# Graph network, one core: block 21 of layer 1 fetched instead of counted, and team pairs of layer 2 moved ahead

## The chip, the cores and the metric

The kernel runs on one core of one Trainium2 chip. The metric is the device time of one execution in microseconds (us), the median over runs. Lower is better.

## The reference

Three graph-convolution layers over 6250 nodes and 100,000 edges (plus one loop per node), then a residual and a layer norm. `norm_edge` is the product of the two ends' `dinv`, so each layer is: scale the rows, sum them over a node's incoming edges, scale again, multiply by a weight matrix, add a bias, relu.

```python
h = x
for W, b in ((W1, b1), (W2, b2), (W3, b3)):      # 256->512, 512->512, 512->256
    h = relu(segment_sum((h @ W)[src] * norm_edge[:, None], dst, num_segments=n) + b)
return layernorm(x + h)
```

## The kernel before

**Blocks, and two ways to sum.** The 6250 nodes are 50 blocks (`NB`) of 125 rows (`Q`). The edges come sorted by destination, so a block's incoming edges are a run of up to 16 chunks of 128 (`KF`). The neighbours' rows of a block are summed in one of two ways.

- *Fetched* ("gathered"): GpSimd (POOL in the profile) issues one indirect DMA per chunk (`gather`, line 1306) that brings 128 source rows, and TensorE (PE) adds them up with a one-hot matrix (`product`, line 1334). Where a row was stored as its fp32r high half and low half side by side (table `both`), one chunk is one matmul over 512 columns. VectorE (DVE) makes the one-hot matrices, four chunks at a time (line 1246), and the last matmul of a block takes the few edges beyond 16 chunks.
- *By count matrix* ("dense"): PE first makes a matrix that holds how many edges lead from each node to each node of the block (`counts`, line 878, from comparisons on DVE in line 811; the banks are copied out as bytes by ScalarE, ACT, in line 840). Then 50 matmuls of 125x125 by 125x512 sum the block (line 1407), one for every block of sources. ACT turns five such 125x125 pieces at a time from bytes to fp32r (line 1255).

Count matrices are made once, in layer 1, for 29 blocks (`MANY`): they are stored to memory and used again in layers 2 and 3.

**Steps.** Each layer is one loop over *steps* in `layer`. A step issues one gather, the product of the gather some steps back, up to three dense matmuls, and whatever the listed generators (`extras`, `going`) have to do in that step. A `yield n` in a generator means "go on n steps later". This order is fixed when the program is built, and each engine runs its part of it in order. Layer 1 is index 0 in the code, layer 2 index 1, layer 3 index 2.

**Layer 1** (451 steps, and a few without a gather at the end). The first 22 blocks (`FEW`) are dense, 28 are fetched; the fetched blocks from `BOTH_FROM` = 26 on come from the table `both`, into 12 row buffers. The dense matmuls are spread over the steps by `spacing`: a block per 19 steps, and never over three matmuls in a step. The count matrices are made in the order of the blocks, with the seven that only later layers use put in behind blocks 3, 6, 9, ... (`EXTRAS_AFTER`). Each summed block goes through `after1`: scale, transpose, W1 (line 1452), bias and relu, and a store to the table of layer 2.

**Teams.** Blocks 0 to 11 of layer 2 are summed by count matrices as three *teams* of four blocks (`teams`). The sum is held transposed in four banks, one a block; for a source block k and a bank, one *pair* of matmuls (high half and low half of k's rows, line 1005) adds its part. There are 3 x 50 x 4 = 600 pairs. They need the rows of layer 2's input, streamed in two blocks at a time (a load for every eight pairs), split by ACT (line 960) and DVE (line 962), and the count pieces, which are loaded and turned to fp32r by ACT (line 952). The pairs begin in layer 1 once the dense blocks are finished, three pairs in two steps, and go on in layer 2: three a step in its first nine steps, then 24 pairs in 23 steps (`PACE`). Counted from the code, the loads for the teams are issued from step 431 on, the first pair stands in step 444, 29 pairs stand in layer 1 and 571 in layer 2, and the last one is in step 532 of layer 2. When a team is complete, DVE scales its four banks (`scaled`, line 940), and `hidden` runs them through W2 and W3.

**Layer 2** (612 steps). Blocks 12 to 49 are fetched, 2 KB a row, into seven row buffers. ACT splits off the high half (line 1366), DVE the low half (line 1371), which sets the row buffer free for the next gather; PE then takes both halves (two matmuls a chunk). `after2` and `hidden` turn two blocks at a time through W2 (line 1513) and W3 (line 1533). Layer 2's first gather needs all of layer 2's table, so it waits for the last block of layer 1 to be stored.

**Layer 3** (322 steps) sums 30 blocks by count matrices and fetches 20.

```python
if in_layer == 0 and pairs_done % 3 or in_layer == 1 and (pairs_done % PACE if now >= EAGER else pairs_done % 3 == 0):
    yield 1
...
until = min(len(work), int((chunk + 1 - first) * NB / spacing))
if i == 0:
    until = min(until, done + 3)
```

Of the kernel before, what the change touches and what calls it, by code (L numbers as in the profile page):

```python
# [31 lines left out]
SOON = 2  # L32
LATE = 6
# [5 lines left out]
SPLIT_ROWS = (12, 9, 20)  # L39
LOANED = 3  # L40
EAGER = 9
PACE = 24
LANDING = 8
AT_ONCE = 3
RETURN = 6
# [5 lines left out]
COUNTING = 3  # L51


FEW = 22
BOTH_FROM = 26
BOTH_LAG = 5
SPLIT = ((0, 0, BOTH_LAG), (1, 2, 8), (0, 0, 10))
EXTRAS_AFTER = (3, 6, 9, 11, 13, 15, 17)
TEAM = 4
TEAMS = 3  # L60
HOME = 17
# [347 lines left out]
def sorted_path(ctx: ExitStack, tc: tile.TileContext, x, edges, starts, found, wts, biases, room, late, out):  # L409
# [60 lines left out]
    def free(name, bank=None):  # L470
        held[name] -= 1
        if name in idle:
            idle[name].append(bank)

    def take(name, most):
        while held.get(name, 0) >= most:
            yield 1
        held[name] = held.get(name, 0) + 1
# [316 lines left out]
    def counts(blocks, places):  # L795
# [4 lines left out]
        def place_for(n):  # L800
            for place in places:
                last = owner.get(id(place))
                if last is None or (last in stored if last >= FEW else last < finished):
                    owner[id(place)] = blocks[n]
# [21 lines left out]
        def copied(now_on):  # L826
            while whole and whole[0][0] <= now_on:
# [5 lines left out]
                stored.add(blocks[n])  # L833
                if blocks[n] < FEW:
                    there.append(now + 1)
# [80 lines left out]
    def teams(groups):  # L916
# [14 lines left out]
        def load(p):  # L931
            if 2 * p < len(units):
                k = units[2 * p][1]
                by_rows(nc.sync, streamed[p % RING], tables[1][k * Q:(k + 2) * Q, :].rearrange("(b p) c -> p b c", p=Q))

        def load_scales(g):
            nc.sync.dma_start(out=scales, in_=dinvs[g * TEAM:(g + 1) * TEAM, :].rearrange("b p -> (b p)").unsqueeze(0).to_broadcast([P, TEAM * Q]))

        def scaled(g, n):
            nc.vector.tensor_tensor(team_zt[:, n], team_banks[n][:, :TEAM * Q], scales, op=ALU.mult)  # L940
            free(f"team{n}")
            if n == TEAM - 1:
                if g + 1 < len(groups):
                    load_scales(g + 1)
                yield SOON
                team_ended[0](hidden(groups[g][:2], team_zt[:, :, :2 * Q], "tz"))
                for _ in range(4 * KF if g + 1 < len(groups) else 2 * KF):
                    yield 1
                team_ended[0](hidden(groups[g][2:], team_zt[:, :, 2 * Q:], "tz"))
# [13 lines left out]

        while products < FEW * NB - HOME // PIECE * PIECE:
            yield 1
# [5 lines left out]
        load_scales(0)  # L971
        while finished < FEW:
            yield 1
# [13 lines left out]
        pairs_done = 0  # L987
        for u, (g, k) in enumerate(units):
            if u == len(units) - RETURN:
                returning = now  # L990
            if u % 2:
                load((u + 1) // 2 + RING - 1)
            for n in range(TEAM):
                if k == 0:
                    yield from take(f"team{n}", 1)
                if k == NB - 1 and n == 0:
                    while held.get("tz", 0):
                        yield 1
                    held["tz"] = TEAM // 2
                if 1 <= n < 3:  # L1000
                    half(u + 2, n - 1)
                if k % PIECE == 2 and u + PIECE < len(units):
                    piece(*divmod(g * CUTS + k // PIECE + 1, CUTS), n)
                for h in range(2):
                    nc.tensor.matmul(team_banks[n][:, :TEAM * Q], lhsT=both_parts[u % 3][:, h * HID + n * P:h * HID + (n + 1) * P],
                                     rhs=team_pieces[(g * CUTS + k // PIECE) % 2][:, k % PIECE, :],
                                     start=(k == h == 0), stop=(k == NB - 1 and h == 1))
                if k == NB - 1:
                    team_ended[0](scaled(g, n))
                pairs_done += 1  # L1010
                if in_layer == 0 and pairs_done % 3 or in_layer == 1 and (pairs_done % PACE if now >= EAGER else pairs_done % 3 == 0):
                    yield 1
        teams_done = True
        assert not on_loan, (now, len(on_loan))
# [142 lines left out]
    def layer(i, width, gathered, dense, after, rows, first=0, spacing=1.0, extras=(), carried=None):  # L1157
# [110 lines left out]
        def of_both(c):  # L1268

            n, b, _ = items[c]  # L1270
            return i == 2 or i == 0 and (n * GRP if b is None else b) >= BOTH_FROM

# [14 lines left out]
        def gather(c):  # L1287
            nonlocal turn
            n, b, j = items[c]
            table = both_halves if i == 0 and of_both(c) else tables[i]  # L1290
            if (i, b, j) == (0, BOTH_FROM, BOTH_LAG + 1):
                hot_stores.appendleft(late_hot_room)
# [313 lines left out]
    now = in_layer = products = 0  # L1606
    few, many, every = list(range(FEW)), list(range(MANY)), list(range(NB))

# [13 lines left out]
    def steps(b):  # L1622

        return (NB - b) * KF + NG - b // GRP
# [8 lines left out]
            yield 1  # L1633

    first = 16
    spacing = 19.0
    made_in_order = []
    for b in few:
        made_in_order.append(b)
        if b in EXTRAS_AFTER:  # L1640
            made_in_order.append(FEW + EXTRAS_AFTER.index(b))
    assert sorted(made_in_order) == many
# [30 lines left out]
    spacing = (steps(len(most)) - SOONER) / (len(most) - BEGUN * PIECE * len(ADVANCE) / NB)  # L1673
# [182 lines left out]
```

## Time and profile before

| what | value |
|---|---|
| median of 3 runs | 2067.19 us (2065.59 to 2067.45) |
| profiled execution, its own time | 2064.83 us |
| its span, first to last instruction | 2063.2 us |
| busy PE / DVE / ACT / POOL | 1926.2 / 1379.0 / 1279.3 / 1381.4 us |
| moved by DMA | 535.53 MB, mean 260 GB/s |

Layer 1's gathers run from 74 to 684 us of the span, layer 2's from 708 to 1615, layer 3's from 1646 to 2049.

In the rows of the profile, "PE" is a matmul, "PEld" the load of its weights, which overlaps other matmuls; matmuls are pipelined too, so the time from the start of one to the start of the next says what it costs, and its own duration does not. In the rows by windows, the number behind x is how many instructions overlap the window. In the timeline, a row is start, duration, engine, line, operation, what it writes and reads, and in brackets the idle time before it with what ended it. A row of waits is: who waited for whom, us in total, times, longest.

### The profile page before, as it was taken

What the parts mean: (1) busy time and instruction counts of PE and PEld (TensorE: products, weight loads), DVE (VectorE), ACT (ScalarE), POOL (GpSimd) and SP (SyncE); (2) the same over time, 40 slices, a digit from 0 to 9 for tenths busy, and PEclk for the clock granted to TensorE, in tenths of its full rate; (3) what the DMA queues carried; (4) which work ended last, traced back from release to release, by engine and by line L of the source; (5) the groups of instructions that cost most, each with busy time, mean ns of one, the idle gap of its engine ahead of it and who ended that gap; (6) DMA issues with size and microseconds to landing.
All of it is one profiled execution on the core that took longest, in us unless ns stands there. A gap on an engine that the chain in (4) does not pass through costs nothing. (4 is left out here: it accounts for less than half of the span.)

```text
span 2063.2 us, 29141 instructions
## 1 busy us (share of the span) xinstructions
PE 1926.2 (93%) x8679; PEld 1521.4 (74%) x8679; DVE 1379.0 (67%) x2443; ACT 1279.3 (62%) x2255; POOL 1381.4 (67%) x1425
## 2 busy tenths in 40 slices
PE   4399999999999789999999989999889999999997
PEld 3277777777777557778888868888768778788886
DVE  6887888887882376677687676767746445444444
ACT  2566777787875466666676666666656555555553
POOL 2467777766777377777676676766757277777775
PEclk9999999999999899999999999999989999999998
DMA  7898999999999998999999998998997599999997
GB/s 171 246 300 220 264 266 259 272 264 254 276 274 248 250 280 255 267 262 265 263 263 265 263 261 249 267 254 253 266 278 221 151 288 292 289 294 299 290 284 203
DMA packets 266078, 535.53 MB, mean 260 GB/s; under 512 B 44363, under 2 KB 80328, under 8 KB 265910
## 3 DMA queue, kind: packets, MB, share of 16 engines
q0 software_dynamic: 155280, 355.58, 63.3%
q1 hardware_dynamic: 97194, 168.45, 30.3%
q10 hardware_dynamic: 13436, 9.55, 1.8%
q8 instruction: 70, 1.15, 0.2%
q14 instruction: 98, 0.80, 0.1%
HBM read 459.56 MB, written 73.87 MB: 259 GB/s over the span
## 5 line engine op out<-in xcount | busy, mean ns | idle before, releaser
L1306 POOL DMA_INDIRECT room<-tab,ssrc x442 | 456.4, 1033 | 199.8 <-issue 86.2
L1334 PE MATMUL sacc<-halves,shot 128*125 128x512 f32 x1524 | 519.9, 402 | 9.7 <-DMA halves<-tab,ssrc 4.7
L1255 ACT CAST piece<-room 125x625 fp32r<-125x625 uint8 x492 | 350.8, 721 | 187.4 <-PE win_ps L1407 53.0
L1306 POOL DMA_INDIRECT halves<-both,ssrc x384 | 360.5, 939 | 141.9 <-issue 42.4
L1306 POOL DMA_INDIRECT halves<-tab,ssrc x320 | 303.2, 947 | 98.8 <-issue 29.2
L1334 PEld LDWEIGHTS sacc<-halves,shot 128*125 128x125 f32 x1524 | 287.1, 189 | 84.3 <-DVE halves L1371 7.5
L811 DVE TENSOR_TENSOR back<-near_cols,slots 128x625 bf16<-128x625 f32 (+2 forms) x435 | 325.0, 803 | 31.5 <-PE sacc L878 12.4
L1371 DVE TENSOR_TENSOR halves<-room,halves 128x512 fp32r<-128x512 f32 x334 | 226.8, 692 | 121.2 <-ACT halves L1366 118.8
L1246 DVE TENSOR_TENSOR shot<-near_cols,sdlo 128x500 fp32r<-128x500 f32 x366 | 244.9, 670 | 93.2 <-PE sacc L1334 87.6
L1306 POOL DMA_INDIRECT back<-tab,ssrc x230 | 230.9, 1004 | 112.9 <-DVE halves L1371 35.1
L1366 ACT CAST halves<-room 128x512 fp32r<-128x512 f32 x334 | 202.0, 620 | 137.8 <-DMA room<-tab,ssrc 127.8
L1513 PE MATMUL win_ps<-back,w_sb 128*128 128x250 f32 x768 | 183.3, 382 | 9.1 <-ACT back L1490 8.6
L1513 PEld LDWEIGHTS win_ps<-back,w_sb 128*128 128x128 f32 x768 | 148.5, 194 | 33.5 <-ACT back L1490 11.0
L1407 PE MATMUL smm<-parts,piece 125*125 125x512 f32 x565 | 165.9, 409 | 2.1 <-DVE parts L1563 1.2
L1407 PE MATMUL win_ps<-parts,piece 125*125 125x512 f32 x550 | 158.2, 406 | 0.0
L1407 PE MATMUL str<-parts,piece 125*125 125x512 f32 x515 | 149.5, 408 | 0.9 <-ACT piece L1255 0.9
L878 PEld LDWEIGHTS <-back 128*125 128x125 bf16 x725 | 95.9, 138 | 73.3 <-issue 23.0
L1407 PE MATMUL sacc<-parts,piece 125*125 125x512 f32 x450 | 147.7, 432 | 0.9 <-ACT piece L1255 0.9
L840 ACT CAST room<-sacc 125x500 uint8<-125x500 f32 (+1 forms) x155 | 107.7, 713 | 55.3 <-PE sacc L878 40.8
L1371 DVE TENSOR_TENSOR halves<-back,halves 128x512 fp32r<-128x512 f32 x136 | 93.3, 693 | 61.1 <-ACT halves L1366 60.4
L1407 PE MATMUL mat_ps<-parts,piece 125*125 125x512 f32 x415 | 121.3, 408 | 0.4 <-ACT piece L1255 0.4
L962 DVE TENSOR_TENSOR parts<-parts 125x512 fp32r<-125x512 f32 x150 | 103.0, 687 | 25.5 <-ACT parts L960 24.8
(353 smaller groups left out, 3477.5 us busy)
## 6 DMA issues: line engine op xcount, KB each, us to landing
parts<-tab SPq DMA_DIRECT2D x75, 448.0 KB
kept<-room SPq DMA_DIRECT2D x29, 683.6 KB
room<-kept SPq DMA_DIRECT2D x27, 683.6 KB
both<-parts SPq DMA_DIRECT2D x10, 1120.0 KB
tab<-st SPq DMA_DIRECT2D x50, 224.0 KB
own_row<-tab SPq DMA_DIRECT2D x38, 224.0 KB
parts<-kept SPq DMA_DIRECT2D x60, 136.7 KB
room<-tab,ssrc POOLq DMA_INDIRECT x442, 6.2
```

The lines of the kernel that those rows point to most:

```text
L811: nc.vector.tensor_tensor(out, near_cols[:, :shape[2]].unsqueeze(1).to_broadcast(shape), numbers.unsqueeze(2).to_broadcast(shape), op=ALU. ...
L840: nc.scalar.copy(place[:, :, u * G:(u + len(ms)) * G].rearrange("p k (t r) -> p t k r", r=G), counted_in[:Q, :len(ms) * 256].rearrange("p ...
L878: nc.tensor.matmul(bank[:Q, len(pair) * 256:][:, :G * NB], lhsT=hot_lo, rhs=hot_key, start=True, stop=True)
L962: nc.vector.tensor_sub(to[:, HID:], row, to[:, :HID].bitcast(F32))
L1246: nc.vector.tensor_tensor(hot[:, :n], near_cols[:, :Q].unsqueeze(1).to_broadcast([P, n, Q]), dlo.rearrange("p b j -> p (b j)")[:, at:at + ...
L1255: nc.scalar.copy(piece[:, :n], made_or_read[:, at:at + n, :])
L1306: nc.gpsimd.indirect_dma_start(out=row, out_offset=None, in_=table, in_offset=bass.IndirectOffsetOnAxis(ap=at, axis=0))
L1334: nc.tensor.matmul(acc[:Q, :size], lhsT=hot, rhs=row[:, c0:c0 + size], start=(i != 0 and k == c0 == 0), stop=(k == KF and c0 + size == row ...
L1366: nc.scalar.copy(halves[:, :width], landed[highs])
L1371: nc.vector.tensor_sub(halves[:, width:], landed.pop(lows), halves[:, :width].bitcast(F32))
L1407: nc.tensor.matmul(acc_d[:Q], lhsT=got[p][:, n, :], rhs=parts[:, k], start=begins and not (i == 2 and m < BEGUN), stop=ends)
L1513: nc.tensor.matmul(h_ps[:, f, :], lhsT=w2_sb[:, k, (f2 + f) * P:(f2 + f + 1) * P], rhs=zt[:, k, :], start=(k == 0), stop=(k == KH - 1))
```

## The change

One block of layer 1, block 21, is fetched instead of summed by its count matrix: 21 dense blocks and 29 fetched ones, 467 steps with a gather instead of 451. `BOTH_FROM` moves with it, so that four blocks are still fetched as plain rows and 25 instead of 24 come from `both`. The count matrix of block 21 is still made, now as the eighth of those for later layers. A dense block is spread over 20 steps instead of 19; 21 x 20 and 22 x 19 are 420 and 418 steps, so the dense blocks end in the same step (435) and the first team pair stands in the same step (444). The 16 further steps lie behind that, with three pairs to two steps: 53 pairs stand in layer 1 and 547 in layer 2. In layer 2, from step 9 on, there is one pair in each step; the last one is in step 530. Behind a finished team, `hidden` of its first two blocks is begun 12 steps after the last scaling instead of 2.

```diff
-FEW = 22
-BOTH_FROM = 26
+FEW = 21
+BOTH_FROM = 25
...
-EXTRAS_AFTER = (3, 6, 9, 11, 13, 15, 17)
+EXTRAS_AFTER = (3, 5, 7, 9, 11, 13, 15, 17)
...
-                yield SOON
+                yield LATE
+                yield LATE
                 team_ended[0](hidden(groups[g][:2], team_zt[:, :, :2 * Q], "tz"))
...
-                if in_layer == 0 and pairs_done % 3 or in_layer == 1 and (pairs_done % PACE if now >= EAGER else pairs_done % 3 == 0):
+                if in_layer == 0 and pairs_done % 3 or in_layer == 1 and (now >= EAGER or pairs_done % 3 == 0):
                     yield 1
...
-    spacing = 19.0
+    spacing = 20.0
```

Three places show how the instructions move. The first is PE in the middle of layer 1, while dense block 4 is summed: `L1407` are the dense matmuls, `L1334` the product of a fetched chunk, `L878` the making of counts. Before:

```order
L878 MATMUL smm<-back 125x250
L1407 MATMUL mat_ps<-parts,piece 125x512 x3
L1334 MATMUL sacc_891<-halves_879,shot_852 125x512
L878 LDWEIGHTS back
L878 MATMUL win_ps<-back 125x250
L1407 MATMUL mat_ps<-parts,piece 125x512 x3
```

Now (line 878 is 877, since a constant is gone):

```order
L1407 MATMUL smm<-parts,piece 125x512 x3
L1334 MATMUL sacc_891<-halves_878,shot_852 125x512
L877 LDWEIGHTS back
L877 MATMUL str<-back 125x250
L877 LDWEIGHTS back
L877 MATMUL sacc_892<-back 125x250
L1407 MATMUL smm<-parts,piece 125x512 x2
```

Two and three dense matmuls now take turns from step to step here, where before three came oftener; elsewhere, where blocks wait for their counts, steps without dense matmuls come in between. The second place is PE at the end of layer 1, at the 18th team pair and what follows: `L1005` is a pair, `L1318` the start of a fetched block, `L1426` a transpose of `after1`. Before:

```order
L1005 MATMUL str<-parts 128x500 x2
L1334 MATMUL win_ps<-halves_880,shot_852 125x512
L1334 MATMUL win_ps<-halves_881,shot_852 125x512
L1005 MATMUL sacc_893<-parts 128x500 x2
L1005 MATMUL mat_ps<-parts 128x500 x2
```

Now, at the same pair:

```order
L1005 MATMUL mat_ps<-parts 128x500 x2
L1005 MATMUL smm<-parts 128x500 x2
L1334 MATMUL sacc_891<-halves_880,shot_853 125x512
L1005 MATMUL str<-parts 128x500 x2
L1334 MATMUL sacc_891<-halves_881,shot_853 125x512
L1426 MATMUL win_ps<-ident_r,szs 128x125 x2
L1005 MATMUL sacc_893<-parts 128x500 x2
L1005 MATMUL mat_ps<-parts 128x500 x2
L1334 MATMUL sacc_891<-halves_870,shot_853 125x512
```

Before, the last products of layer 1 stood there and only pairs and the last block's `after1` came behind them; now a whole fetched block still follows, with the pairs between its products.

The third place is PE in layer 2 at the product of its 19th and 20th chunks (two matmuls each), where the old pace put two pairs in one step. Before:

```order
L1334 MATMUL sacc_892<-halves_6034,shot_853 125x512 x2
L1005 MATMUL str<-parts 128x500 x2
L1005 MATMUL sacc_893<-parts 128x500 x2
L1334 MATMUL sacc_892<-halves_6035,shot_853 125x512 x2
L1005 MATMUL mat_ps<-parts 128x500 x2
```

Now:

```order
L1334 MATMUL sacc_892<-halves_6084,shot_852 125x512 x2
L1005 MATMUL str<-parts 128x500 x2
L1334 MATMUL sacc_892<-halves_6085,shot_852 125x512 x2
L1005 MATMUL sacc_893<-parts 128x500 x2
```

The second pair of that step is gone, and so in every 23rd step of layer 2.

1 line of the change is left out of this document (removed).

## Prediction

> **What bounds the kernel now.** I read the page for its totals, then the windows by stage, then what each engine waits for in a stage, and last the timeline at the end of layer 1, where the change puts its work. First the page, and the windows: layer 1's steady stretch, its end, layer 2's steady stretch, layer 3.
>
> ```profile
> PE 1926.2 (93%) x8679; PEld 1521.4 (74%) x8679; DVE 1379.0 (67%) x2443; ACT 1279.3 (62%) x2255; POOL 1381.4 (67%) x1425
> ```
>
> ```profile
> core 0: us, PE busy (x) PEld busy (x) DVE busy (x) ACT busy (x) POOL busy (x), PEclk, DMA share, GB/s
> 74.00:160.00 86.00, 68.02 (x325) 51.51 (x326) 69.76 (x119) 49.60 (x85) 55.74 (x56) 1.00 0.85 267
> 232.00:640.00 408.00, 402.86 (x1930) 298.51 (x1929) 334.41 (x546) 315.98 (x556) 292.39 (x311) 1.00 0.96 265
> 900.00:1480.00 580.00, 566.69 (x2546) 471.06 (x2545) 424.77 (x676) 387.78 (x713) 404.38 (x395) 0.99 0.92 261
> 1646.00:2050.00 404.00, 401.72 (x1730) 320.66 (x1728) 195.98 (x474) 210.38 (x333) 304.58 (x322) 1.00 1.16 286
> ```
>
> PE is busy almost throughout in all three, but a busy PE may still be waited for or not, so the steps and the waits decide. The same windows for the gathers alone count the steps, and the waits of POOL in layer 1 say what holds them:
>
> ```profile
> 232.00:640.00 408.00, 288.74 (x308) 1.00 0.96 265
> 1646.00:2050.00 404.00, 304.58 (x322) 1.00 1.16 286
> ```
>
> ```profile
> POOL halves L1306 <- PE sacc L1334: 14.3, 30, 1.4
> POOL halves L1306 <- PE sacc L878: 14.1, 31, 2.0
> ```
>
> Layer 1 takes 408/308 = 1.325 us a step. Layer 3 takes 404/322 = 1.255, and the timeline of POOL shows why no layer can go below that by much: gathers that nothing holds up start 1.24 us apart (674.55, 675.79).
>
> ```profile
> 655.50 0.94 POOL L1306 DMA_INDIRECT halves<-both,ssrc  x1 [0.30 <-PE smm L1334]
> ...
> 674.55 0.94 POOL L1306 DMA_INDIRECT halves<-both,ssrc  x1 [0.30 <-issue]
> 675.79 0.94 POOL L1306 DMA_INDIRECT halves<-both,ssrc  x1 [0.31 <-issue]
> ...
> 684.37 0.94 POOL L1306 DMA_INDIRECT halves<-both,ssrc  x1 [2.67 <-DMA parts<-tab]
> 708.49 1.01 POOL L1306 DMA_INDIRECT room<-tab,rest  x1 [23.18 <-ACT parts L960]
> ```
>
> So in layer 1 PE sets the pace (POOL's waits name PE, which hands the row buffers back), 0.08 us a step above POOL's floor; in layer 3 PE and that floor lie together; and between 684.37 and 708.49 POOL has nothing to do until the last block of layer 1 is through.
>
> **The change, term by term.** The profiled execution took 2064.83 us, 2.4 below the median of 2067.19; the sum is made against the former and 2.4 is added at the end.
>
> *First term: 50 dense matmuls leave layer 1's steady stretch.* What one costs shows where nothing else is between them:
>
> ```profile
> 637.01 0.40 PE L1334 MATMUL sacc<-halves,shot 128*125 128x512 f32 x1
> 637.24 0.87 PE L1407 MATMUL win_ps<-parts,piece 125*125 125x512 f32 x3
> 637.96 0.39 PE L1334 MATMUL sacc<-halves,shot 128*125 128x512 f32 x1
> ```
>
> Four matmuls of 512 columns in 637.96 - 637.01 = 0.95 us: 0.235 each, not the 0.39 of the row. 50 x 0.235 = 11.7 us. The dense work ends in the same step (435), so this comes off the same number of steps. Up to about step 58 PE is not full (68 of 86 us in the window from 74), and 43 x (50/19 - 50/20) = 6 of the 50 fall there; 44 x 0.235 = 10.3. Spread over 377 steps that is 0.027 a step, to 1.298, still above 1.24, so POOL's floor does not take it back. I take -10; bounds -5 (if half of the steps without a dense matmul run into that floor) and -11.7. The ten casts to fp32r that go from ACT, and the gather rate that rises by 2% from 265 GB/s where layer 3 moves 286, I cost at nothing: neither ACT nor the transfers hold PE there.
>
> *Second term: 16 more steps at the end of layer 1*, each with a gather of 256 KB, a product and one and a half pairs. The timeline of PE (and one row of ACT) over that end:
>
> ```profile
> 676.18 0.50 PE L1334 MATMUL win_ps<-halves,shot 128*125 128x512 f32 x1 [2.91 <-DMA halves<-both,ssrc]
> 676.77 0.62 ACT L960 CAST parts<-parts 125x512 fp32r<-125x512 f32 x1 [6.07 <-DMA parts<-tab]
> 680.77 2.07 PE L1452 MATMUL sacc<-w,back 128*125 128x512 f32 x2 [4.08 <-ACT back L1446]
> ...
> 687.74 0.40 PE L1334 MATMUL win_ps<-halves,shot 128*125 128x512 f32 x1
> 687.98 0.62 PE L1005 MATMUL sacc<-parts 125*128 125x500 f32 x2
> 688.44 0.40 PE L1334 MATMUL win_ps<-halves,shot 128*125 128x512 f32 x1
> 688.68 0.61 PE L1005 MATMUL mat_ps<-parts 125*128 125x500 f32 x2
> 689.13 0.61 PE L1005 MATMUL smm<-parts 125*128 125x500 f32 x2
> 689.58 0.39 PE L1334 MATMUL win_ps<-halves,shot 128*125 128x512 f32 x1
> ...
> 695.05 0.62 PE L1334 MATMUL win_ps<-halves,shot 128*125 128x512 f32 x2
> ```
>
> ```profile
> 676.00:686.00 10.00, 5.73 (x9) 3.01 (x10) 2.13 (x4) 4.98 (x9) 5.41 (x6) 0.53 1.33 284
> ```
>
> At the first pairs PE stands still (2.91 and 4.08 us), since ACT waits 6.07 us for the rows streamed in for the teams, and it comes back at half its clock (0.53). That costs what it did: it lies ahead of the added steps. Then two steps take 689.58 - 687.74 = 1.84 us on PE, 0.92 a step. Sixteen are 14.7; one more block's turn through `after1` falls among them, four matmuls at W1, which I estimate at twice the price of a 512-column matmul each, 1.9. PE alone makes that 16.6. By POOL's floor it is 16 x 1.24 = 19.8 for the gathers, but PE trails at the end now: its last product starts 10.7 us behind the last gather's issue, while a gather lands sooner than that:
>
> ```profile
> halves<-both,ssrc POOLq DMA_INDIRECT x384, 4.8
> ```
>
> With 0.94 + 4.8 = 5.7 us instead of 10.7, 19.8 becomes 14.9. The larger of the two prices, 16.6, counts; with the streams of 24 more pairs beside the gathers I take +17. Bounds: +15, and +23 if the added steps go at the pace of the last twenty gathers, (684.37 - 655.50)/20 = 1.44. The last block's `after1` and its store behind the last product are unchanged.
>
> *Third term: 24 pairs leave layer 2.* A pair is 689.13 - 688.68 = 0.45 us of PE; 24 are 10.9. Whether layer 2's steps are PE's is not as plain:
>
> ```profile
> 900.00:1480.00 580.00, 404.38 (x395) 0.99 0.92 261
> ```
>
> ```profile
> PE sacc L1005 <- DVE back L940: 6.4, 2, 5.3
> ...
> ACT halves L1366 <- DMA room<-tab,ssrc: 72.8, 57, 4.8
> ...
> ACT back L1521 <- PE win_ps L1513: 21.2, 11, 3.7
> ...
> DVE halves L1371 <- ACT halves L1366: 104.6, 102, 4.3
> ...
> POOL room L1306 <- DVE halves L1371: 42.0, 59, 2.7
> ```
>
> 580/395 = 1.468 us a step, and PE's longest total wait is 6.4 us: PE is full, and less work on it should tell. But POOL waits for DVE, DVE for ACT, and ACT mostly for the rows to land; that circle through seven row buffers names PE little (21.2 us). Bounds: 0 (the circle sets the pace) and -10.9. I take -8, nearer to PE, because it is busy in 566.69 of 580 us. What goes with the pairs, three stream loads and the casts for them, helps the circle a little and is in that value.
>
> *At nothing:* the 12 steps instead of 2 ahead of a team's `hidden` hold up no engine, only the place where its instructions are written; the next team's end needs them over 190 steps later. Order and number of the count matrices: 29 as before, all made by the same step. Layer 3 is untouched.
>
> Sum: -10 + 17 - 8 = -1; 2063.8 against the profiled execution, **2066.2 us** against the median. 0.2% (4.1 us) is about what a measurement of this kernel can tell from no change; within it lie 2063.1 to 2071.3.
>
> **The rivals.**
>
> *PE sets every stage (faster).* Then all 50 matmuls and all 24 pairs count and the end of layer 1 costs its lower bound: -11.7 + 15 - 10.9 = -7.6, 2059.6 us. For it: PE's busy time, its few waits, the POOL waits that name it. Against: the circle in layer 2, and the early steps.
>
> *The circle of gathers sets layer 2 (slower).* A row lands, ACT and DVE split it, POOL may fetch again; with fewer pairs PE only waits more. The third term is then 0: -10 + 17 = +7, 2074.2 us. It decides if the pace in layer 2's 521 one-pair steps falls by less than 3/521 = 0.006 us. For it: 104.6 us of DVE on ACT and 72.8 of ACT on landing rows. Against: PE's 98% there.
>
> *Layer 1's steady stretch is not PE's (slower).* If PE had room there, 50 matmuls fewer would change no step: 17 - 8 = +9, 2076.2 us. For it speaks the weight loads' 298.51 of 408 us, 73%. The Trainium skill, Perfetto Trace Analysis, Identifying the Most-Contended Engine, holds that matmul busy time is no measure of a full TensorE and that the busy share of weight loads is to be read instead; by that rule this stretch has a quarter of PE to spare, and the sum would be the one just given. Against: POOL's waits name PE, and where dense matmuls follow each other they start every 0.235 us with no gap.
>
> That the change moves something else than it says is excluded by the order: the dense work ends in the same step, and the pairs stand where they should.
>
> **How the numbers follow.** The terms as sized: 0.38, 2062 to 2071. PE everywhere: 0.36, 2056 to 2063. The circle in layer 2: 0.20, 2071 to 2077. Layer 1's steady stretch not PE's: 0.06, 2073 to 2080. So faster 0.36, same 0.38, slower 0.26. From 2056 to 2077 nearly all of the first three are held and some of the last, with room for terms off on the same side; as the terms' bounds reach further (from -7.6 to +18), I leave it there for 8 in 10.
>
> **What would show it.** Right: layer 1's steady steps near 1.30 us with about the same 308 gathers in some 400 us; the last gather of layer 1 about 10 us later than 684.37; layer 2's first gather near 715; layer 2's steady steps near 1.453; layer 3 at 404 us as now. Wrong: steady steps of layer 1 still at 1.325 (the first term), POOL waits in the added steps beyond 1.24 that name transfers (the second), or layer 2's steps at 1.468 with longer PE waits for splits (the third).

## The result and the profile after

The changed kernel takes 2074.68 us (median of 11 runs), the kernel before 2065.59 on the same chip: ratio 1.0055, interval 1.0041 to 1.0069, so 8 to 14 us slower. The profiled execution took 2073.48 us, its span is 2071.8 against 2063.2. The forecast was no change.

First the windows of the changed kernel, all engines for the steady stretches of layers 1 and 2, then the gathers alone:

```profile
232.00:640.00 408.00, 402.01 (x1934) 297.91 (x1933) 336.62 (x549) 315.44 (x556) 301.52 (x321) 1.00 0.98 272
900.00:1480.00 580.00, 565.78 (x2531) 467.77 (x2530) 423.40 (x673) 387.17 (x713) 412.24 (x398) 0.99 0.92 260
```

```profile
232.00:640.00 408.00, 297.86 (x318) 1.00 0.98 272
900.00:1480.00 580.00, 412.24 (x398) 0.99 0.92 260
```

Layer 1 now fits 318 gathers into the 408 us that held 308: 1.283 us a step instead of 1.325. Layer 2 fits 398 instead of 395 into 580. Both moved the forecast way. The loss is at the end of layer 1. POOL's timeline there, from gather 430 (counted from 0; it stood at 655.50 before) to layer 2's first:

```profile
643.19 0.94 POOL L1306 DMA_INDIRECT halves<-both,ssrc  x1 [0.30 <-PE sacc L1407]
...
668.77 0.94 POOL L1306 DMA_INDIRECT halves<-both,ssrc  x1 [0.30 <-issue]
680.06 0.94 POOL L1306 DMA_INDIRECT halves<-both,ssrc  x1 [10.35 <-PE sacc L1334]
...
702.42 1.01 POOL L1306 DMA_INDIRECT halves<-both,ssrc  x1 [0.30 <-issue]
724.26 0.95 POOL L1306 DMA_INDIRECT room<-tab,rest  x1 [20.82 <-DMA parts<-tab]
```

From gather 430 to layer 2's first gather, 708.49 - 655.50 = 53.0 us became 724.26 - 643.19 = 81.1: 28.1 more, where the second term had 17. In the middle POOL waits 10.35 us for PE to give a row buffer back. Following that wait back, in the same stretch of the timeline, one row each of DVE, ACT and PE:

```profile
674.70 0.69 DVE L1457 TENSOR_TENSOR st<-win_ps,back 125x512 f32<-125x512 f32 x1 [13.16 <-DMA tab<-st]
...
675.43 0.72 ACT L1460 ACTIVATE st<-st,sdinv 125x512 f32<-125x512 f32 x1 [12.31 <-DVE st L1457]
...
676.46 2.07 PE L1452 MATMUL win_ps<-w,back 128*125 128x512 f32 x2 [10.06 <-ACT back L1446]
```

PE waits for ACT, ACT for DVE's bias add in `after1`, and DVE for a store to land, since there are two store buffers and both still have theirs outstanding. Why the store is late, SP's queue shows. The changed kernel:

```profile
643.14 4.50 SPq L86 DMA_DIRECT2D parts<-kept  x8
649.42 3.05 SPq L86 DMA_DIRECT2D parts<-tab  x6
652.99 13.58 SPq L86 DMA_DIRECT2D parts<-kept  x8
667.18 0.35 SPq L936 DMA_DIRECT2D room<-dinvs  x1
667.64 16.12 SPq L84 DMA_DIRECT2D tab<-st  x8
```

and the kernel before:

```profile
648.71 15.79 SPq L85 DMA_DIRECT2D tab<-st  x8
664.59 4.16 SPq L87 DMA_DIRECT2D parts<-kept  x8
668.85 3.62 SPq L87 DMA_DIRECT2D parts<-tab  x6
673.15 11.41 SPq L87 DMA_DIRECT2D parts<-kept  x8
685.48 0.35 SPq L937 DMA_DIRECT2D room<-dinvs  x1
685.93 2.64 SPq L85 DMA_DIRECT2D tab<-st  x4
```

`parts<-kept` and `parts<-tab` are the teams' loads of matrices and streamed rows, `tab<-st` the stores of `after1`, two DMAs a block. Before, four blocks' stores in this view stand ahead of the loads and two blocks' behind; now four blocks' stand behind, and the first is issued at 667.64, some 24 us after the loads began. Of DVE's 13.16 us, some 6 lie ahead of that issue and 7 between it and the landing.

The lengths of these rows are not what the issues themselves take: one issue took 0.30 to 0.45 us. In between SP waits, as the waits of its queue from 625 to 690 us say (the changed kernel):

```profile
SPq L84 <- ACT st L1460: 15.4, 2, 9.4
SPq L84 <- ACT back L1446: 13.9, 2, 7.6
SPq L86 <- DMA parts<-tab: 10.9, 4, 4.9
```

Among the loads, by the profile, it mostly waits until streamed rows have landed. Of the 16.12 us of the eight stores, 12.3 are waits for ACT, in two gaps (6.0 and 6.3 us): the later of these stores wait for `after1`, which the stall itself holds up. So that row is long because of the stall and did not cause it. What moved the stores is a rule that the diff doesn't touch: `ended` hurries the steps of `after1` only from step `total - 2 * KF` on. With 16 more steps that is 435 instead of 419, while the team loads stay at step 430, so two blocks that used to be hurried past the loads no longer are.

### The profile page after: what moved, and what is told of

It reads as the page before. It is cut to its first block, busy times and chain, and to the rows that moved or that the text cites. A ratio compares the mean times of both kernels' runs of the same rounds, so it can differ in the third digit from the quotient of the medians.

```text
span 2071.8 us, 29085 instructions
## 1 busy us (share of the span) xinstructions
PE 1922.3 (93%) x8648; PEld 1514.1 (73%) x8648; DVE 1381.0 (67%) x2448; ACT 1273.7 (61%) x2245; POOL 1403.0 (68%) x1441
## 2 busy tenths in 40 slices
DMA packets 268382, 539.73 MB, mean 261 GB/s; under 512 B 44619, under 2 KB 80584, under 8 KB 268214
## 4 chain that ended last, share of the span: by engine, by line
PE 52%; DMA 22%; issue 10%; POOL 8%; DVE 4%; ACT 3%; SPq 1%; ACTq 0%; POOLq 0%; DVEq 0%
DMA room<-tab,ssrc 11%; PE sacc L1334 9%; PE smm L1407 7%; PE win_ps L1407 6%; POOL room L1306 5%; PE str L1407 5%; DMA back<-tab,ssrc 5%; PE mat_ps L1407 5%; PE sacc L1407 4%; POOL back L1306 2%; PE win_ps L1513 2%; DMA own_row<-tab 2%; PE sacc L877 1%; DVE back L810 1%; PE win_ps L1533 1%
## 5 line engine op out<-in xcount | busy, mean ns | idle before, releaser
L1306 POOL DMA_INDIRECT room<-tab,ssrc x442 | 458.6, 1037 | 203.0 <-issue 84.4
L1334 PE MATMUL sacc<-halves,shot 128*125 128x512 f32 x1624 | 561.1, 404 | 11.6 <-DMA halves<-both,ssrc 3.6
L1306 POOL DMA_INDIRECT halves<-both,ssrc x400 | 376.7, 942 | 144.6 <-issue 34.8
L1255 ACT CAST piece<-room 125x625 fp32r<-125x625 uint8 x482 | 343.7, 721 | 185.0 <-PE win_ps L1407 50.3
L1334 PEld LDWEIGHTS sacc<-halves,shot 128*125 128x125 f32 x1624 | 305.6, 188 | 95.5 <-DVE halves L1371 7.4
L810 DVE TENSOR_TENSOR back<-near_cols,slots 128x625 bf16<-128x625 f32 (+2 forms) x435 | 324.2, 802 | 27.1 <-PE sacc L877 10.5
L1407 PE MATMUL smm<-parts,piece 125*125 125x512 f32 x665 | 198.4, 412 | 2.1 <-DVE parts L1563 1.2
L1407 PE MATMUL win_ps<-parts,piece 125*125 125x512 f32 x550 | 156.7, 403 | 0.0
L1407 PEld LDWEIGHTS smm<-parts,piece 125*125 125x125 f32 x665 | 115.9, 187 | 29.4 <-issue 4.5
L1407 PE MATMUL str<-parts,piece 125*125 125x512 f32 x465 | 133.5, 405 | 0.0
L1407 PE MATMUL mat_ps<-parts,piece 125*125 125x512 f32 x415 | 122.2, 409 | 0.0
```

Source lines behind the costliest of these rows:

```text
L810: nc.vector.tensor_tensor(out, near_cols[:, :shape[2]].unsqueeze(1).to_broadcast(shape), numbers.unsqueeze(2).to_broadcast(shape), op=ALU. ...
L1255: nc.scalar.copy(piece[:, :n], made_or_read[:, at:at + n, :])
L1306: nc.gpsimd.indirect_dma_start(out=row, out_offset=None, in_=table, in_offset=bass.IndirectOffsetOnAxis(ap=at, axis=0))
L1334: nc.tensor.matmul(acc[:Q, :size], lhsT=hot, rhs=row[:, c0:c0 + size], start=(i != 0 and k == c0 == 0), stop=(k == KF and c0 + size == row ...
L1407: nc.tensor.matmul(acc_d[:Q], lhsT=got[p][:, n, :], rhs=parts[:, k], start=begins and not (i == 2 and m < BEGUN), stop=ends)
```

## The experiments

**Theory A**: the order on SP's queue makes the added wait. **Theory B**: the end of layer 1 is short of bandwidth, and the order doesn't matter. For the other 20 us: the pace of gathers that nothing holds up, 1.243 us from one to the next (their floor), against PE's work with the added pairs. For layer 2: PE against the circle of gathers and splits, in which POOL waits for a row buffer, DVE for ACT, and ACT for the rows to land.

One thing is needed to read the runs: they were made in six sessions, each with the kernel before beside them, and in four of these every stage of every kernel, before included, took about 10% longer (before: 2260 to 2289 us). There layer 1's steady stretch runs at 1.48 to 1.52 us a step, whatever the number of matmuls. Ratios are therefore read within a session, and the causes of the first result from sessions 3 and 4, and from single rows. Each stage time in the table is that of one profiled execution.

| kernel | session (its before, us) | ratio to before, interval | gather 430 to layer 1's last, us | to layer 2's first | layer 2, first to last gather |
|---|---|---|---|---|---|
| before (profile of the prediction) | | | 28.9 | 53.0 | 906.3 |
| changed (result above) | (2065.59) | 1.0055, 1.0041-1.0069 | 59.2 | 81.1 | 901.3 |
| stores on ACT's queue | 1 (2280.24) | 1.0117, 1.0080-1.0153 | 54.2 | 75.1 | 980.4 |
| hurried earlier | 1 | 1.0109, 1.0065-1.0153 | 55.0 | 77.8 | 983.7 |
| before, two stores later | 1 | 1.0012, 0.9989-1.0035 | 34.0 | 57.3 | 974.8 |
| before, 22 pairs less | 1 | 1.0005, 0.9981-1.0028 | 33.4 | 57.1 | 978.3 |
| changed | 2 (2259.98) | 1.0150, 1.0121-1.0178 | 60.2 | 84.1 | 971.6 |
| stores on ACT's queue | 2 | 1.0167, 1.0134-1.0200 | 56.5 | 79.5 | 972.0 |
| hurried earlier | 2 | 1.0167, 1.0137-1.0196 | 55.1 | 79.1 | 972.6 |
| before, two stores later | 2 | 1.0012, 0.9990-1.0034 | 33.6 | 57.5 | 963.5 |
| before, two stores on ACT | 3 (2065.29) | 0.9990, 0.9969-1.0011 | 30.1 | 53.3 | 906.3 |
| stores on ACT's queue | 4 (2064.84) | 1.0039, 1.0021-1.0057 | 52.2 | 73.4 | 907.2 |
| hurried earlier | 4 | 1.0039, 1.0023-1.0056 | 52.3 | 75.1 | 909.9 |
| before, two stores later | 4 | 1.0015, 0.9999-1.0031 | 34.0 | 57.5 | 905.8 |
| before, 22 pairs less | 4 | 0.9987, 0.9971-1.0003 | 30.7 | 54.2 | 906.1 |
| changed | 5 (2288.71) | 1.0126, 1.0093-1.0159 | 58.1 | 79.2 | 987.4 |
| old rule for pairs | 5 | 1.0201, 1.0164-1.0239 | 57.4 | 78.4 | 991.9 |
| 22 pairs less at the end | 5 | 1.0112, 1.0080-1.0144 | 53.5 | 76.3 | 995.0 |
| 23 blocks | 5 | 1.0005, 0.9980-1.0029 | | | 991.8 |
| 23 blocks | 6 (2264.24) | 0.9954, 0.9927-0.9982 | | | 978.2 |

**The stores of five blocks on ACT's queue** (of the changed kernel):

```
-        by_rows(nc.scalar if b == NB - 1 else nc.sync, y, ...
+        by_rows(nc.scalar if b in (19, 20, 46, 47, 48, NB - 1) else nc.sync, y, ...
```

> The changed kernel, with the stores of the after-steps of blocks 19, 20, 46, 47 and 48 issued from ACT's queue instead of SP's. Theory A (these stores stand behind the second team's loads of matrices and dinvs on SP's in-order queue; the third bias add of an after-step then waits for a store's landing, ACT for the add, PE for ACT, the gathers for PE): the 10.06 us for which PE waits on ACT L1446 at the end of layer 1 go, layer 2's first gather starts near 714 us instead of 724.26, and the time is about 10 us under the changed kernel's 2074.68, near 2064.5. Theory B (the end of layer 1 is short of DMA bandwidth, with 16 more steps of gathers beside the team's loads; the order on the queue doesn't matter): layer 2's first gather stays at 722 to 726 and the time within 3 us of 2074.7.

> Again the changed kernel with the stores of blocks 19, 20, 46, 47 and 48 on ACT's queue, since the first try was on a chip where every stage was 10% longer and layer 1's steady stretch (1.50 us a step with 50 matmuls more or fewer) wasn't set by PE. Theory A: the 10-us wait of PE on ACT L1446 goes, from the 430th gather to the last of layer 1 it takes about 49 instead of 59 us, and the time is 8 to 12 us under the changed kernel's on this chip. Theory B: within 3 us of it.

> The changed kernel with the stores of blocks 19, 20, 46, 47 and 48 on ACT's queue, tried again where the gathers come every 1.24 us and layer 1's steady stretch is PE's (the two tries before ran 10% longer in every stage). Theory A: from the 430th gather to the last of layer 1 some 49 instead of 59.2 us, the wait of PE on ACT L1446 of 10.06 us gone, ratio to before 0.999 to 1.002 instead of 1.0055. Theory B: 57 to 61 us, ratio 1.004 to 1.007.

(What these texts call the second team's loads are the first team's in the code, `fetch_counts(0, 0)` and what follows it.)

What engines wait for between 640 and 726 us, in the changed kernel:

```profile
ACT st L1460 <- DVE st L1457: 21.3, 6, 12.3
...
POOL halves L1306 <- PE sacc L1334: 15.0, 7, 10.3
DVE st L1457 <- DMA tab<-st: 13.2, 1, 13.2
...
PE win_ps L1452 <- ACT back L1446: 10.1, 1, 10.1
```

and with the stores on ACT's queue, session 4:

```profile
ACT st L1460 <- DVE st L1457: 9.4, 5, 4.0
POOL halves L1306 <- PE sacc L1334: 8.5, 8, 4.7
...
PE win_ps L1452 <- ACT back L1446: 5.1, 1, 5.1
...
DVE st L1457 <- DMA tab<-st: 3.3, 1, 3.3
```

Gather 430, layer 1's last and layer 2's first, in the same run:

```profile
643.96 0.94 POOL L1306 DMA_INDIRECT halves<-both,ssrc  x1 [0.30 <-PE sacc L1407]
...
696.20 1.41 POOL L1306 DMA_INDIRECT halves<-both,ssrc  x1 [0.30 <-issue]
717.34 0.95 POOL L1306 DMA_INDIRECT room<-tab,rest  x1 [19.73 <-DMA parts<-tab]
```

DVE's wait for a store falls from 13.2 to 3.3 us, PE's for ACT from 10.1 to 5.1, near the 4.08 that it was before the change, and the stretch from gather 430 to the last of layer 1 from 59.2 to 52.2. So the order on the queue costs 7 us there: theory A holds in place and mechanism, with 7 us where 10 were expected. The Trainium skill (DMA: Bandwidth & Descriptors, Issuing engines are not separate DMA queues) holds that issuing from several engines saves only the time that the issuing takes, usually little beside the transfer. That an issue by itself is small agrees with this trace (0.30 to 0.45 us). But more than issues was saved here, 7 us of the stretch: on a queue of their own the stores no longer stand behind SP's waits. The time of the whole follows less: 1.0039 instead of the expected 0.999 to 1.002, with intervals that overlap those of the changed kernel, and in session 2 no gain at all (1.0167 beside 1.0150) though the stretch was 3.7 us shorter. In session 4 layer 2 took 907.2 us against 901.3, though not an instruction of it differs. So the 7 us are shown for the stretch, and not for the whole time.

**The after-steps hurried earlier** (of the changed kernel), the second way of restoring the order:

```
-            most = LATE if chunk < total - 2 * KF else 1
+            most = LATE if chunk < total - (3 if i == 0 else 2) * KF else 1
...
+        yield 1
         fetch_counts(0, 0)
```

> The changed kernel, with the after-steps of layer 1 hurried from step 419 on (as before the change) instead of from 435, and the second team's fetch one step later, so that the stores of blocks 19 and 46 stand ahead of that fetch on SP's queue, and those of 20, 21, 47 and 48 no later than they stood before the change. Theory A: the wait of 10.06 us goes as in the run with the stores on ACT's queue; layer 2's first gather near 714 to 716, time 2064 to 2067. Theory B: no stream is smaller and no gather fewer, so 722 to 726 and within 3 us of 2074.7. If the hurried chains themselves crowd PE, up to 2 us of the gain are lost.

> Again the changed kernel with the after-steps of layer 1 hurried from step 419 and the second team's fetch one step later. Theory A: from the 430th gather to the last of layer 1 about 49 to 51 instead of 59 us, 7 to 11 us under the changed kernel's time on this chip, so level with before or up to 3 us faster. Theory B: within 3 us of the changed kernel.

> The changed kernel with the after-steps of layer 1 hurried from step 419 and the second team's fetch one step later, so that the stores of blocks 19 and 46 stand ahead of the loads. Theory A: from the 430th gather to the last of layer 1 some 49 to 51 us, ratio to before 0.999 to 1.002. Theory B: 57 to 61 us, ratio 1.004 to 1.007.

The same waits, session 4:

```profile
ACT parts L960 <- DMA parts<-tab: 22.5, 5, 9.6
...
ACT st L1461 <- DVE st L1458: 11.0, 4, 4.4
...
PE win_ps L1453 <- ACT back L1447: 7.7, 1, 7.7
```

and the gathers:

```profile
643.44 0.94 POOL L1307 DMA_INDIRECT halves<-both,ssrc  x1 [0.31 <-PE sacc L1427]
...
695.73 0.94 POOL L1307 DMA_INDIRECT halves<-both,ssrc  x1 [0.30 <-issue]
718.50 0.95 POOL L1307 DMA_INDIRECT room<-tab,rest  x1 [21.84 <-DMA parts<-tab]
```

DVE's wait for a store is gone from the list, and the stretch is 52.3 us, as with ACT's queue: two different edits, which share that the early stores no longer stand behind the loads on SP, agree within 0.1 us. The time is 1.0039 again, where 0.999 to 1.002 was expected. What is left is the stall that was there before the change, ACT waiting for the streamed rows; it holds PE for 7.7 us now instead of 4.08. Whether that is a lack of bandwidth, as theory B has it, no run here shows.

**The kernel before with two stores later**: nothing of the change in it, but four blocks' stores behind the loads.

```
+        if b in (20, 47):
+            yield 1
         by_rows(nc.scalar if b == NB - 1 else nc.sync, y, ...
```

> The kernel before, with one more step ahead of the stores of blocks 20 and 47, so that these two stores come one step behind the second team's fetch instead of with it: four stores then stand behind the loads on SP's queue, as after the change; steps, pairs and matmuls are those of before. Theory A: a third bias add waits for a landing as in the changed kernel, the last gather of layer 1 comes 5 to 10 us later than 684.37 and the time is 5 to 10 us over before's. Theory B: nothing moves, within 2 us of before, last gather of layer 1 at 683 to 687.

> Again the kernel before with the stores of blocks 20 and 47 one step later, behind the second team's fetch on SP's queue. Theory A: from the 430th gather to the last of layer 1 it takes 5 to 10 us longer than the 28.9 us of before, and the time is as much over before's. Theory B: within 2 us of before.

> The kernel before with the stores of blocks 20 and 47 one step later, behind the second team's fetch. On the two chips where all took 10% longer nothing moved (1.0012). Theory A: from the 430th gather to the last of layer 1 5 to 10 us more than 28.9, ratio 1.0025 to 1.005. Theory B, or A with the wait hidden because these two are the last but one of their chains: no change, 0.999 to 1.001.

Timeline of session 4, a row of POOL and one of DVE:

```profile
682.63 0.94 POOL L1306 DMA_INDIRECT halves<-both,ssrc  x1 [7.17 <-PE win_ps L1334]
```

```profile
677.28 0.69 DVE L1457 TENSOR_TENSOR st<-sacc,back 125x512 f32<-125x512 f32 x1 [12.90 <-DMA tab<-st]
```

One step's delay of two stores brings the 12.90-us wait into a kernel that hadn't got it. The stretch takes 34.0 us, against 28.9 to 30.7 in the three profiles of sessions at the short pace that leave these two stores in place: 3 to 5 us, where theory A gave 5 to 10. In sessions 1 and 2 the edit brings a wait of 10.0 us into the same place, but there the stretch says nothing: 34.0 us beside 33.4 for the kernel of session 1 that leaves layer 1 alone. The whole time is 1.0015, from no change to 6 us more; 1.0025 to 1.005 was expected, so the size is missed, but it is the same wait in the same place.

**The kernel before with stores of blocks 21 and 48 on ACT's queue**, the control:

```
-        by_rows(nc.scalar if b == NB - 1 else nc.sync, y, ...
+        by_rows(nc.scalar if b in (21, 48, NB - 1) else nc.sync, y, ...
```

> The kernel before, with the stores of blocks 21 and 48, the two that stand behind the second team's loads on SP's queue there, issued from ACT's queue: the control of the run with five stores on ACT. Theory A: before the change only two stores stand behind the loads, and the wait they cost is the 2.9 and 4.1 us of the first pairs at most, so 0 to 4 us less than before. Theory B: nothing moves, within 2 us.

0.9990 (0.9969 to 1.0011), no difference that shows; the stretch is 30.1 us. The two stores that stood behind the loads before the change cost nothing that shows, and putting stores on ACT's queue gains nothing by itself here.

**The kernel before without 22 pairs of layer 2**:

```
-                for h in range(2):
+                for h in range(0 if in_layer == 1 and now >= EAGER and 0 < k < NB - 1 and pairs_done % PACE == 0 else 2):
```

> The kernel before, without the 22 second team pairs of a step in layer 2: their rows are left out of the sums, so this is work left out and not a version. Layer 1 is untouched. If PE sets layer 2 throughout, 22 x 0.45 = 9.9 us go from layer 2's 906.3 us between its first and last gather; by the prediction's third term, scaled from 24 to 22 pairs, 7.3 us; if the circle of gathers and products sets it, 0 to 1 us. The changed kernel's trace (906.3 to 901.3) speaks for about 5.

> The kernel before without the 22 second team pairs of a step in layer 2 (their rows are left out of the sums). If PE sets layer 2 throughout: 9.9 us less from its first gather to its last (906.3), ratio 0.995; by the prediction's third term 7.3 us; if the circle of gathers and products sets it, 0 to 1 us. The changed kernel's layer 2 (901.3) speaks for about 5.

The window of session 4, all engines (all of POOL's 394 are gathers), then the waits in the same window, then layer 2's first and last gather:

```profile
900.00:1480.00 580.00, 559.29 (x2490) 461.49 (x2489) 420.97 (x672) 386.63 (x712) 410.15 (x394) 0.99 0.92 260
```

```profile
DVE halves L1371 <- ACT halves L1366: 98.8, 102, 4.0
ACT halves L1366 <- DMA room<-tab,ssrc: 75.5, 63, 4.9
```

```profile
708.01 1.29 POOL L1306 DMA_INDIRECT room<-tab,rest  x1 [22.65 <-ACT parts L960]
...
1614.09 0.94 POOL L1306 DMA_INDIRECT back<-tab,ssrc  x1 [0.72 <-DVE halves L1371]
```

PE is busy 7.4 us less than the 566.69 of before, and the window holds 394 gathers instead of 395; from first to last gather layer 2 takes 906.1 us instead of 906.3. ACT waits for the rows (75.5 us, 72.8 before) and DVE for ACT (98.8, 104.6) as ever. So PE does not set layer 2's pace, though before the change it is busy in 98% of that window. That the circle sets it is what is left; no run here shortened the circle itself. The time, 0.9987 with 0.9971 as its lower end, speaks against the 9.9 us (0.9952) and the 7.3 (0.9965) as well, the latter by little. In session 1 it was 1.0005.

**The old rule for pairs in the changed kernel**, and the changed kernel again as yardstick:

```
-                if in_layer == 0 and pairs_done % 3 or in_layer == 1 and (now >= EAGER or pairs_done % 3 == 0):
+                if in_layer == 0 and pairs_done % 3 or in_layer == 1 and (pairs_done % 24 if now >= EAGER else pairs_done % 3 == 0):
```

> The changed kernel as it is, as the yardstick for the runs beside it on the same chip. If this chip paces the gathers as the first comparison did (1.24 us from one to the next for 7 of 10, steady stretch of layer 1 near 1.29): ratio 1.004 to 1.007 over before, last gather of layer 1 near 702, layer 2's first near 724. If it paces them as the chip of the first four experiments (1.50): no gain from 50 matmuls less, 16 steps more at 1.5, about 24 us over before, 1.011.

> The changed kernel as it is, a second time where the gathers come every 1.24 us: the yardstick for the three beside it, and whether its layer 2 (901.3 us from first to last gather, against 906.3 before and 907.2 and 909.9 in the two kernels that differ from it in layer 1 alone) is a gain of the pairs or chance. A gain of the pairs: again 900 to 903. Chance: 905 to 910. From the 430th gather to layer 2's first again 79 to 83 us; ratio to before 1.004 to 1.007.

> The changed kernel with the rule for team pairs in layer 2 of before: every 24th pair shares a step, the blocks split 21 to 29 as in the change. The prediction's third term and the theory that PE sets layer 2: the share of the gain that goes with 20-odd doubled pairs is lost or moves, up to 5 us in layer 2 against the changed kernel. Circle theory (borne out by the run with 22 pairs less, 906.1 against 906.3): layer 2 as in the changed kernel within 2 us, ratio within 0.001 of it.

Session 5 was a long one, so whether the 901.3 us are chance wasn't answered. In session 2 the yardstick missed its own forecast: 1.0150 (1.0121 to 1.0178), where 1.011 was expected at that pace. Within session 5 the old rule is slower than the changed kernel, 1.0201 against 1.0126, with intervals that just don't meet (six runs each, medians 2329.25 and 2317.54 us); its profile puts 4.5 us of that in layer 2, and the circle theory had allowed 2 us and 0.001. In session 4 leaving out such pairs' matmuls in the kernel before changed nothing, so PE's work is unlikely to be the reason; something else goes with a doubled pair (its stream loads and casts come earlier too). No run shows which.

**22 of the 53 pairs left out at the end of layer 1**, with the five stores on ACT's queue. The expectation says 24, but the edit's `0 < k` keeps the two that fall on k = 0, and the trace has 44 matmuls of line 1005 fewer, 1156 instead of 1200:

```
-                for h in range(2):
+                for h in range(0 if in_layer == 0 and pairs_done % 2 and pairs_done < 48 and 0 < k < NB - 1 else 2):
```

> The changed kernel with five stores on ACT's queue and without 24 of the 53 team pairs at the end of layer 1 (every second of the first 48; their rows are left out of the sums): the added pairs are gone, the 16 added steps with their gathers stay. If PE sets the added steps (the prediction's second term took 16.6 of PE and 24 pairs): from the 430th gather to layer 2's first 73.3 us fall by 24 x 0.45 = 10.8. If the gathers' floor sets them (16 x 1.243 = 19.9): no more than 2 us less.

Gather 430, then layer 1's last and layer 2's first:

```profile
724.95 0.94 POOL L1306 DMA_INDIRECT halves<-both,ssrc  x1 [0.30 <-issue]
...
778.49 0.94 POOL L1306 DMA_INDIRECT halves<-both,ssrc  x1 [0.30 <-DMA parts<-tab]
801.27 0.95 POOL L1306 DMA_INDIRECT room<-tab,rest  x1 [21.84 <-DMA parts<-tab]
```

76.3 us to layer 2's first gather, where the same kernel with all its pairs took 75.1 and 79.5 in the other long sessions. Of the 22 x 0.45 = 9.9 us that the pairs would be if PE set these steps, between none and 3 are there. So the gathers set them: 16 x 1.243 = 19.9 us. This compares sessions at the long pace; at the short one the gathers' starts say the same. With all pairs and the stores on ACT's queue (session 4), 27 of the 36 gathers behind gather 430 come within 1.30 us of the one before, and the gaps beyond 1.243 add up to 7.5 us, where before they added up to 4.0 over 20 gathers.

**The change turned round**: 23 blocks by count matrices.

```
-PACE = 24
+PACE = 8
...
-FEW = 22
-BOTH_FROM = 26
+FEW = 23
+BOTH_FROM = 27
...
-EXTRAS_AFTER = (3, 6, 9, 11, 13, 15, 17)
+EXTRAS_AFTER = (4, 8, 11, 13, 15, 17)
...
-    spacing = 19.0
+    spacing = 18.0
```

> The change turned round: 23 blocks by count matrices and 27 fetched, every 8th team pair of layer 2 doubled so that the teams still end in time (PACE 8 instead of 24). If an added fetched block costs 16 gathers at their floor at the end of layer 1 and saves 9 to 10 us in its steady stretch, and pairs in layer 2 are free: 20 less at the end, 10 more in the steady stretch, layer 2 as before, so about 10 us under before, ratio 0.995. If PE sets layer 2, its added pairs take 24 x 0.45 = 10.8 back: ratio 1.000. If the matmuls added to the steady stretch cost more than they saved, slower than before.

> The change turned round (23 blocks by count matrices, 27 fetched, every 8th team pair of layer 2 doubled), again, since the first try was on a chip where layer 1's steady stretch isn't PE's. By the stages measured so far: one fetched block less takes 16 gathers, 20 us, off the end of layer 1 and about 9 to 10 us come back in the steady stretch, so layer 2's first gather comes about 10 us earlier than 708.5; if layer 2 keeps its 906 us, ratio 0.995. If the added pairs, or what they move, lengthen layer 2 by 10 us or more (the first try's layer 2 had one gap of 12.7 us), ratio 1.000 or above.

Steady stretch of layer 1, gathers alone: the changed kernel (21 blocks) in session 5,

```profile
232.00:640.00 408.00, 254.54 (x271) 0.97 0.85 232
```

and 23 blocks in session 6:

```profile
232.00:640.00 408.00, 255.95 (x273) 0.98 0.87 233
```

Two blocks' dense matmuls more or fewer make no difference to the pace at the long pace (within session 5 it is 1.506 and 1.508 us a step), so there the 16 gathers that go cost nothing elsewhere in layer 1: 0.9954 in session 6. In session 5 it was 1.0005, against the 0.995 expected; the two intervals barely touch. Both profiles have a long gap in layer 2 at the same gather, 12.7 and 9.3 us from one to the next; POOL's row in session 6:

```profile
1347.99 0.94 POOL L1306 DMA_INDIRECT room<-tab,ssrc  x1 [8.33 <-DVE parts L1371]
```

So at the long pace turning the change round is no slower than before, and in one session of two 0.5% faster. It didn't run in a session where before takes 2065 us, and the gap in layer 2 was not worked on; both are open.

## Why the prediction was wrong

**First term, right in size.** From the first gather to gather 430 the change gained 581.8 - 571.4 = 10.4 us; -10 was forecast. All four profiles of before and its variants at the short pace give 575.0 to 581.8, the three of the changed kind 568.6 to 571.4. Counted from the starts of the gathers between 232 and 640 us, the gaps beyond 1.243 us add up to 25.8 us before (22.6 to 25.8 in the four profiles) and to 14.0 now: what went is waiting of POOL, which its rows put mostly to PE. No run separates the 50 matmuls from the wider spacing and the new order of the count matrices, so that it is their number alone isn't shown. The rival by which this stretch is not PE's (the Trainium skill, Perfetto Trace Analysis, Identifying the Most-Contended Engine: read the weight loads' share, and beside it the share of the peak arithmetic, which no trace here gives) fell here: the loads' share is 297.91 of 408 us, 73% as before, and yet with fewer matmuls the stretch was shorter. In the long sessions it came true: there the stretch up to gather 430 took as long with 50 matmuls less, and the ratio was 1.0126 and 1.0150.

**Second term, where it failed.** Forecast +17, measured +28.1. The step that failed is "That costs what it did: it lies ahead of the added steps". The stall at the first pairs did not keep its length, since the 16 added steps postpone the hurried steps of `after1` past the team loads; PE's wait for ACT there went from 4.08 to 10.06 us. With it falls the sentence that anything else moving "is excluded by the order": the stores did move. The edits that take the stores out from behind the loads bring 28.1 down to 20.4 and 22.1, so 6 to 8 us hang on it. The sum had looked at where the pairs and products stand, and not at where a rule written as "so many steps before the end" moves the stores against loads that don't move.

The rest of the term, 20 to 22 us, is inside the bounds of +15 to +23 but came out by the other price. The prediction took PE's 16.6 over the gathers' 14.9; the gathers set it, at 19.9, and PE's 24 pairs cost little or nothing. The catch-up of 5 us that was taken off was 24.1 - 21.8 = 2.3 us between the last gather of layer 1 and the first of layer 2. Together: 19.9 for 16 gathers at 1.243, 10.5 for gaps beyond that (14.5 us behind gather 430, 4.0 before), less 2.3, is the 28.1 measured.

**Third term, wrong in its reason.** -8 was forecast from PE's 98%; without 22 of the pairs layer 2 stays at 906.1 us. The rival of the circle was right that fewer pairs gain nothing there. The changed kernel's own layer 2 is 5.0 us shorter, but the same instructions took 907.2 and 909.9 in the two kernels that differ from it in layer 1, so no gain of the pairs is shown. In session 2 the three changed kernels took 971.6 to 972.6 us for layer 2, and the variant of before 963.5.

**The sum** as the two profiles have it: -1.9 up to the first gather, -10.4, +28.1, -5.0, and -2.2 from layer 2's last gather on: +8.6 us, the difference of the spans. That the circle rival's 2074.2 lies beside the 2074.68 measured is half chance: it had the third term at zero, but kept +17 for the second. That the measured time lies inside 2056 to 2077 is luck as well: the second term was 11 us too small, and 1.9 and 2.2 us at the two ends of the kernel, which no term had, took some of it back.

**What stays open.** Where the 6 to 8 us went that the two kernels with the stores moved gained ahead of layer 2: their times are 1.0039 against 1.0055, some 3 us, and layer 2 took 6 to 9 us more in their profiles. The times can't tell a part given back from scatter.

## What to carry to other kernels

When a change lengthens a stage, look for every rule that counts from the end of the stage, and see which small stores now stand behind large loads on an in-order queue; a store that nobody reads soon can still hold an engine through its buffer, as the two store buffers did here. That an engine is busy 98% of a stage doesn't show that it sets the pace; leaving out some of its work is a cheap way to see.

## What the runs showed of the hardware

SP issued in the order of the program, and what waited held up what stood behind it: one issue took 0.30 to 0.45 us, but from the first team load to the first store behind the loads 24.5 us went by (643.14 to 667.64). DVE waited 13.16 us for that store to land, and PE, at the end of the chain, 10.06 us.

The same program can run at another pace in another session, on one and the same chip: the kernel before took 2280.24 us in session 1 and 2064.84 in session 4, both on one chip. The gathers' own duration hardly changed (the largest group of them: 1037 ns in the changed kernel's first profile, 1048 in session 5), nor did the volume (539.73 MB in both). What grew is idle time, much of which the profile puts to no releaser. That says less than it seems: the traces at the long pace hold 16,256 to 17,531 semaphore updates, those at the short pace 45,253 to 45,687, so releasers may be missing from the record. The mean granted clock was 0.939 to 0.969 in the long profiles and 0.962 to 0.987 in the short ones; the ranges overlap. The cause of the long pace is not known. It decides what a change is worth: 50 matmuls fewer went with 10 us less at one pace and with nothing at the other.
